# Grouping the scores of the first two quads and the sums of one graph, with six feature blocks moved by ScalarE: a fused graph-attention and relational-attention kernel

## The chip, the core and the metric

The kernel runs on one core of a Trainium2 chip, in one launch. The metric is the device time of that launch in microseconds; less is better. The core has five engines that this document speaks of: TensorE (PE in the profile; PEld is its weight loading), VectorE (DVE), ScalarE (ACT), GpSimd (POOL) and SyncE (SP), which here only issues DMAs. Each works through its own queue in order and waits on semaphores for the others.

## What is computed

Two layers over 64 graphs of 256 nodes with 256 features, all in 32-bit floating point. `adj` holds 0 or 1.

```python
# layer 0: two graph-attention passes, residual, norm, feed-forward, norm
def _gat(h, adj, W, a, n):
    Wh = h @ W
    e = leaky_relu(Wh @ a[:n] + swapaxes(Wh @ a[n:], 1, 2), 0.2)
    return softmax(where(adj > 0, e, -9e15), axis=1) @ Wh
h = _gat(_gat(x, adj, W1, a1, 256), adj, W2, a2, 256)
h = layernorm(x + h) * g_ln1 + b_ln1
x = layernorm(h + relu(h @ w_ff1 + b_ff1) @ w_ff2 + b_ff2) * g_ln2 + b_ln2

# layer 1: eight heads of 32 features; values depend on the relation r = adj
q, k = heads(x @ Wq + bq), heads(x @ Wk + bk)
attn = softmax(q @ k.T / sqrt(32))
out = sum((attn * (adj == r)) @ heads(x @ Wv[r] + bv[r]) for r in range(4))
x1 = layernorm(x + merge(out) @ Wo + bo) * g1 + beta1
x = layernorm(x1 + gelu(x1 @ W1 + b1) @ W2 + b2) * g2 + beta2
```

## The kernel before

The path that runs (`narrow_path`) uses that the adjacency of these inputs holds only 0 and 1, so relational attention needs two value projections. (`general_path` stands in the file for other inputs; it is not run here.) Two graphs make a unit of 512 rows (`G = 2`, `T = 4` tiles of 128 rows), so there are 32 units (`NG`). One call of `turn(y_, x_, z)` works on three units at once: unit `y_` is in relational attention and its feed-forward, unit `x_` in the feed-forward of layer 0, unit `z` in its graph attention. There are 32 turns. In turns 0 to 30 there is a unit `x_` (`X` in the code is true); in turns 1 to 30 the code calls the turn `middle`. In the last turn there is none.

Inside a turn the order of TensorE, SyncE, VectorE and ScalarE is written by hand (`tc.manual_schedule`): each queue holds the instructions in the order of the source. GpSimd's order is left to the scheduler.

Large products use a seven-product scheme in place of eight block products (as Strassen's): a step `2`, `1`, `5`, `3`, `6`, `7` or `4` is one block product, accumulated in PSUM and taken out after each step. What takes it out is ScalarE (a copy) where an output quarter is written first, and VectorE (an add) where the quarter has been begun. This holds for the projections and for the hidden layer:

- `p("q2 v2 q1 ...")` runs steps of the projections of unit `y_`: `q` stands for queries and keys together, `v` for the values. Steps 2, 5 and 3 share one bank, steps 1, 6, 7 and 4 another. The value projections use two banks of their own, with the tags `zo` and `po`. The evictions are on L1040 (VectorE) and L1043 (ScalarE).
- `first("2a 1a ...")` runs steps of the hidden layer of unit `x_`, on halves `a` and `b`. Steps 2, 5 and 3 of a half share the bank `h1b`, steps 1, 6, 7 and 4 the bank `h1a`. The adds are on L909, the copies on L912. `ra`, `rb`, `sa`, `sb` are activations on ScalarE. Steps 5, 6, 7 and 4 need differences of the features, `tt` (L882, four subtractions on VectorE).

PSUM has eight banks of 128 x 512: six of the tag `g`, which `bank()` hands out, and one each of `zo` and `po`.

Attention goes by quads: quad n is four heads of one of the two graphs, so a unit has four quads, 0 and 1 of the first graph, 2 and 3 of the second. For a quad,

- `scores(n)` makes four score tiles on TensorE (L1076, tile `sp`), one bank for each head, with 32 rows of the array for each head, and then calls `powers`;
- `powers(n, heads)` is the exponential on ScalarE (L1085, tile `e`), which frees the bank; `e` and its masked copy `ea` have two buffers each;
- `masks(n)` multiplies by the adjacency on VectorE (L1089, tile `ea`), in two instructions of two heads;
- `totals(n)` adds the two node blocks on VectorE (L1094, tile `es`);
- `sums(n)` makes the weighted values (L1104, tile `po`) and the softmax denominators (L1107, tile `zo`) on TensorE, 32 columns of the array for each head; one bank of each tag serves both quads of a graph;
- `shares(b)` divides, on VectorE (`rz`, `rq`, then L1124), and `out_(b)` is the output projection (`yop`, L812).

In a middle turn TensorE's order around the change is: `q2 v2 q1 v1 q5`, scores 0, `v5 q6 v6 q3 q7 v7 v3 q4 v4`, scores 1, sums 0, `2a 1a 5a`, scores 2, sums 1, scores 3, then `6a 3a` and the other steps of the hidden layer, two products of unit `z` (`xpp`, L741) and step `4b`, sums 2, sums 3, `yop`.

`normed_features` turns a normalized unit into feature-major layout: VectorE transposes blocks of 32 x 32 (`yt`, L694), and 16 blocks of 32 x 256 are then moved between partition groups into `hT`. Four stay in their group (GpSimd). The other twelve are moved by DMAs from SyncE's queue (L714) in the call for layer 0's feed-forward; in the later call for layer 1's feed-forward eight of the twelve are copies by ScalarE (`n % 3 in (1, 2)`).

Other pieces named later: `applied_norm` (L856) is the normalization on ScalarE, four instructions a unit; `offsets` (L846, tile `nm`) prepares its bias; `moments` are the statistics on VectorE (L827, L828); `times` and `plus` (L865, L868) are the scale and shift by the rows `rg` and `rb`; `early(z)` is a transpose for unit `z` (L1135).

Of the kernel before, what the change touches and what calls it, by code (L numbers as in the profile page):

```python
# [9 lines left out]
F32 = mybir.dt.float32  # L10
# [6 lines left out]
P = 128  # L17
# [368 lines left out]
def narrow_path(  # L386
# [13 lines left out]
    nc = tc.nc  # L400
# [8 lines left out]
    T = G * NB  # L409
# [13 lines left out]
    def bank(name):  # L423
        return psum.tile([P, 512], F32, tag="g", name=name, bufs=6)
# [261 lines left out]
        nc.gpsimd.memset(hT[KB - 1][one], 1.0)  # L686
        return hT

    def normed_features(u, l, xn, natural=False, copied=()):


        yt = work.tile([P, Q, KB, T, 32], F32, tag="yt", name=f"yt{u}_{l}", bufs=1)
        for t in range(T):
            mark["transposed"] = nc.vector.transpose(  # L694
                yt[:, :, :, t].rearrange("p q k r -> p k q r"),
                xn[:, t].rearrange("p (k q c) -> p k q c", k=KB, c=32))
        if natural:
            hT = work.tile([P, KB, TN], F32, tag="hT", name=f"hT{u}_{l}")
            to = hT.rearrange("c k (t a r) -> c (k t) a r", a=Q, r=32)
            for q in reversed(range(Q)):  # L700
                for a in range(Q):
                    move = nc.gpsimd.tensor_copy if q == a else nc.sync.dma_start
                    move(to[q * 32:(q + 1) * 32, :, a], yt[a * 32:(a + 1) * 32, q].rearrange("c k t r -> c (k t) r"))
            return with_ones([hT[:, k] for k in range(KB)])
        hT = work.tile([P, Q, KB, T, 32], F32, tag="hT", name=f"hT{u}_{l}")
        n = 0
        for q in range(Q):
            for a in range(Q):
                to, at = hT[q * 32:(q + 1) * 32, a], yt[a * 32:(a + 1) * 32, q]
                if q == a:  # L710
                    nc.gpsimd.tensor_copy(to, at)  # L711
                else:
                    move = nc.scalar.copy if n % 3 in copied else nc.sync.dma_start
                    mark["placed"] = move(to, at)  # L714
                    n += 1
        return [hT[:, :, k].rearrange("p a t r -> p t a r") for k in range(KB)]

    def early_first(z):

# [128 lines left out]
    def applied_norm(y, blocks, mv, rs, nm, part=None, gpsimd=False):  # L848
        if part is None:
            offsets(blocks, mv, rs, nm)  # L850
        for t in part or blocks:
            if gpsimd:
                nc.gpsimd.tensor_scalar(y[:, t, :], y[:, t, :], rs[:, t:t + 1], nm[:, t:t + 1],
                                        op0=ALU.mult, op1=ALU.add)
                continue
            mark["normed"] = nc.scalar.activation(y[:, t, :], y[:, t, :], AF.Identity,  # L856
                                                  bias=nm[:, t:t + 1], scale=rs[:, t:t + 1])
# [6 lines left out]
    def times(y, g_):  # L864
        nc.vector.tensor_mul(y, y, g_[:, None, :].to_broadcast(list(y.shape)))  # L865
# [198 lines left out]

    isd = 1.0 / math.sqrt(DH)

    def weighted(u, b, m, q, k_, aT):


        n = f"{u}_{b}_{m}"  # L1070
        ps = [bank(f"sp{n}_{a}") for a in range(HPB)]
        for j in range(NB):
            j0 = b * N + j * P
            for a in range(HPB):
                hp = slice(a * DH, (a + 1) * DH)
                nc.tensor.matmul(ps[a][:, j * N:(j + 1) * N], k_[hp, m, j0:j0 + P],  # L1076
                                 q[hp, m, b * N:(b + 1) * N], start=True, stop=True)
        e = work.tile([P, HPB, NB * N], F32, tag="e", name=f"e{n}")
        ea = work.tile([P, HPB, NB * N], F32, tag="ea", name=f"ea{n}")
        ab = aT[:, b * NB:(b + 1) * NB, :].rearrange("p t n -> p (t n)")  # L1080
        return ps, (b, m, ab, e, ea)
# [136 lines left out]
    def piece():  # L1218
        if left:
            next(left[0], None)  # L1220

    def turn(y_, x_, z):
# [8 lines left out]
        e, pe = {}, {}  # L1231

        def scores(n, heads=range(HPB)):
            pe[n], e[n] = weighted(y_, *quads[n], q, k_, Y["aT"])
            powers(n, heads)

        def powers(n, heads):
            exps(pe[n], *e[n], heads)

        def masks(n, *pairs):  # L1240
            masked(*e[n], *pairs)

        def totals(n):
            e[n] = node_sums(*e[n])
# [15 lines left out]
            add_blocks(y_, "yop", y, b, lambda t, k: oT[:, k, t * P:(t + 1) * P],  # L1260
                       lambda b, k: wo[:, k, :], KB)

        def first(names, ends=0):

            if X:
                steps(names)
            else:
                for _ in range(ends):
                    piece()


        order = tc.manual_schedule(engines={getattr(mybir.EngineType, n) for n in
                                            ("PE", "SP", "DVE", "Activation")[:4 if X else 2]})
        with order:
# [2 lines left out]
                n = X.pop("n")  # L1277
                offsets(*n)
            middle = X and y_
            p("q2 v2 q1 v1" if middle else "q1 v1 q2")  # L1280
            if middle:
                applied_norm(X["y"], *n, [0, 1, 2, 3])
            elif X:
                applied_norm(X["y"], *n, [0])
            if not middle:
                p("v2")
            if X and not middle:
                applied_norm(X["y"], *n, [1])
            if not middle:
                p("q5")  # L1290
            if X and not middle:
                applied_norm(X["y"], *n, [2, 3])
            if X:
                X["hT"] = normed_features(x_, 0, X["y"])
            if middle:
                p("q5")
                scores(0, (0, 1))
            else:
                scores(0, (0,))
                p("v5")  # L1300
                powers(0, (1,))
            if z + 1 < NG:
                load_x(z + 1)
            if waiting:
                w, wy = waiting[0]
                last = moments(w, 3, wy, range(NB))
            p("v5 q6" if middle else "q3 v3")
            if middle:
                powers(0, (2,))
                p("v6")  # L1310
                powers(0, (3,))
            else:
                powers(0, (2, 3))
            if X:
                masks(0, (0,))
            if middle:
                times(X["y"], rg1)
                p("q3 q7 v7")
                masks(0, (2,))
            else:  # L1320
                p("q6 v6 q7 v7")
                if X:
                    masks(0, (2,))
            if X:
                totals(0)
            else:
                with behind("projected"):
                    masks(0)
                    totals(0)
            while late:  # L1330
                affine(*late.pop(0))
            p("v3 q4 v4" if middle else "q4 v4")
            if waiting:
                last = norm(w, 3, wy, mv=last)
            steps = first_hidden(x_) if X else None
            scores(1)
            masks(1, (0,))
            if waiting:
                offsets(*last)
            masks(1, (2,))  # L1340
            totals(1)
            sums(0)
            if waiting:
                first("2a 1a")
                applied_norm(wy, *last, [0, 1])
                first("5a")
            else:
                first("2a 1a 5a", 1)
            if Z:
                early(z)  # L1350
            scores(2)
            sums(1)
            if waiting:
                applied_norm(wy, *last, [2, 3])
            scores(3, (0, 1, 2))
            first("6a")
            powers(3, (3,))
            if X:
                masks(2)
                totals(2)  # L1360
            first("3a", 1)
            if not X:
                with behind("out"):
                    shares(0)
                masks(2)
                totals(2)
            first("2b ra")
            if X:
                shares(0, [0])
            first("1b 7a")  # L1370
            if X:
                shares(0, [1])
            first("5b sa 6b 4a")
            masks(3, (0,))
            first("3b rb 7b")
            first("sb", 2)
            masks(3, (2,))
            totals(3)
            if X:
                if not middle:  # L1380
                    times(X["y"], rg1)
                plus(X["y"], rb1)
            if Z:
                project(z, range(0, T // 2))
            first("4b")
            sums(2)
            sums(3)
            if not Z:
                shares(1)
            if X:  # L1390
# [51 lines left out]
                Z["m"].scaled(WH)  # L1442
            if Z:
                out.product(6)
                hT = normed_features(y_, 2, y, copied=(1, 2))
                nc.scalar.activation(work.tile([P, 1], F32, tag="ve", name=f"ve{y_}"), mhalf[:, 0:1], AF.Gelu)
                out.add(6)
                out.sums(3)
                out(3)
            elif X:  # L1450
                out.sums(4)
                out(7, 3)
# [191 lines left out]
```

## Time and profile before

| what | value |
|---|---|
| median of 3 runs | 2977.74 us (2977.12 to 2978.61) |
| the profiled execution's own time | 2977.29 us |
| its span | 2975.6 us |
| busy: TensorE | 2936.1 us (99%) |
| busy: VectorE | 2624.7 us (88%) |
| busy: ScalarE | 1822.6 us (61%) |
| busy: GpSimd | 635.6 us (21%) |
| one middle turn | 90.26 us (first projection at 1008.87 us and, a turn later, at 1099.13 us) |
| exponential, 128 x 512, on ScalarE (L1085) | 606 ns, 512 times |
| mask, 128 x 1024, on VectorE (L1089) | 1211 ns, 256 times |
| block move, 32 x 256, on ScalarE (L714) | 402 ns, 240 times |

Times in views are microseconds from the start of the span. A busy time counts an instruction from its start to its end; on VectorE and ScalarE the next instruction may start some 0.1 us before the one ahead is at its end, so the distance from start to start is what a queue advances by. Ends on TensorE are modelled, and its chain lists the distance from one group to the next.

### The profile page before, as it was taken

To read this page: it belongs to the slowest core of one execution; us is meant where nothing else is said; L and a number is where in the kernel's file an instruction comes from. 1 tells how busy PE (TensorE), PEld (TensorE's weight loads), DVE (VectorE), ACT (ScalarE), POOL (GpSimd) and SP (SyncE) were. 2 spreads that over 40 slices of the span, in tenths; PEclk is the share of its full clock that TensorE was granted. 3 is DMA by queue.
4 is the path that set the end of the run, shared out by engine and by line. 5 is a ranking of instruction groups with operands and counts; after the bars stand their busy time and mean duration, and the time that the engine had idled before them with its cause. 6 is when DMAs were issued, how large, how long until landed. Compare 5 with 4: busy or idle time off the path is not lost.

```text
span 2975.6 us, 58457 instructions
## 1 busy us (share of the span) xinstructions
PE 2936.1 (99%) x22192; PEld 2501.2 (84%) x22192; DVE 2624.7 (88%) x5024; ACT 1822.6 (61%) x3803; POOL 635.6 (21%) x930
## 2 busy tenths in 40 slices
PE   7999999999999999999999999999999999999997
PEld 6788888888888888888888888888888888888876
DVE  5788999988999989898989999889999898989886
ACT  4466666656656666666666666666566566666653
POOL 4122121221211221211221212212112212112211
PEclk8999999999999999999999999999999999999999
DMA  5011111111111111111111112111112111111000
GB/s 151 14 32 34 36 33 26 42 35 37 35 34 28 42 35 37 32 26 40 39 35 35 33 26 42 35 36 35 36 26 42 35 37 32 27 38 35 19 10 16
DMA packets 416883, 105.36 MB, mean 35 GB/s; under 512 B 360746, under 2 KB 416084, under 8 KB 416596
## 3 DMA queue, kind: packets, MB, share of 16 engines
q1 hardware_dynamic: 415196, 100.23, 15.5%
q8 instruction: 177, 2.90, 0.4%
q0 software_dynamic: 1056, 1.05, 0.1%
q14 instruction: 110, 0.90, 0.1%
q10 hardware_dynamic: 344, 0.28, 0.0%
HBM read 56.78 MB, written 16.78 MB: 25 GB/s over the span
## 4 chain that ended last, share of the span: by engine, by line
PE 96%; DVE 2%; ACT 1%; DMA 1%; issue 0%; POOL 0%; SPq 0%; POOLq 0%; DVEq 0%; ACTq 0%
PE yf L989 26%; PE h1a L900 15%; PE h1b L900 11%; PE po L1104 8%; PE v L1056 7%; PE qk L1056 6%; PE sp L1076 5%; PE yop L812 4%; PE xpp L741 4%; PE hpp L801 4%; PE ygp L812 3%; PE zo L1107 2%; PE rows L750 1%; DMA wf<-in_L_gnn_w_ff_dram 0%; DVE s L776 0%
## 5 line engine op out<-in xcount | busy, mean ns | idle before, releaser
L1089 DVE TENSOR_TENSOR ea<-e,aT 128x1024 f32<-128x1024 f32 x256 | 307.0, 1211 | 4.2 <-ACT e L1085 4.2
L1085 ACT ACTIVATE e<-sp 128x512 f32<-128x512 f32 x512 | 277.2, 606 | 51.7 <-PE sp L1076 35.8
L856 ACT ACTIVATE y<-y,nm,rs 128x256 f32<-128x256 f32 x450 | 243.1, 596 | 98.9 <-DVE nm L846 94.2
L912 ACT COPY h<-h1b 128x512 f32<-128x512 f32 x262 | 152.7, 583 | 192.7 <-PE h1b L900 191.0
L711 POOL COPY hT<-yt 32x256 f32<-32x256 f32 x244 | 237.4, 973 | 139.0 <-DVE yt L694 131.4
L1043 ACT COPY qk<-qk 128x512 f32<-128x512 f32 x128 | 74.3, 581 | 290.4 <-PE qk L1056 289.0
L918 ACT ACTIVATE h<-h,cols 128x256 f32<-128x256 f32 x512 | 220.8, 498 | 31.4 <-DVE h L909 31.4
L909 DVE TENSOR_TENSOR h<-h1a,h 128x512 f32<-128x512 f32 x262 | 176.2, 682 | 53.1 <-PE h1a L900 43.7
L838 POOL TENSOR_SCALAR rs<-mv 128x4 f32<-128x4 f32 (+1 forms) x134 | 33.9, 253 | 872.4 <-DVE mv L828 296.7
L997 DVE TENSOR_TENSOR y<-yf,y 128x256 f32<-128x256 f32 x448 | 185.5, 414 | 34.0 <-PE yf L989 33.7
L827 DVE BATCH_NORM_STATS2 st<-y 128x6 f32<-128x256 f32 x512 | 208.3, 409 | 5.6
L1117 POOL TENSOR_TENSOR low<-low,rq 128x16 f32<-128x16 f32 x64 | 13.9, 217 | 781.8 <-DVE rq L1116 781.8
L743 ACT COPY xp<-xpp 128x260 f32<-128x260 f32 x128 | 44.2, 368 | 212.0 <-PE xpp L741 211.9
L868 DVE TENSOR_TENSOR y<-y,rb 128x1024 f32<-128x1024 f32 (+1 forms) x130 | 166.0, 1277 | 2.2
L865 DVE TENSOR_TENSOR y<-y,rg 128x1024 f32<-128x1024 f32 (+1 forms) x130 | 162.0, 1246 | 1.2 <-ACT y L856 1.1
L1094 DVE TENSOR_TENSOR es<-e 128x1024 f32<-128x1024 f32 x128 | 155.7, 1217 | 0.0
L1076 PE MATMUL sp<-qk 32*128 32x256 f32 x2048 | 146.6, 400 | 0.0
L1104 PE MATMUL po<-e,v 128*32 128x256 f32 x2048 | 136.3, 384 | 2.1 <-DVE qk L1124 2.1
L839 POOL TENSOR_TENSOR rs<-rs,mhalf 128x4 f32<-128x4 f32 (+1 forms) x134 | 134.6, 1004 | 8.4
L1104 PE MATMUL po<-ea,v 128*32 128x256 f32 x2048 | 134.0, 379 | 0.0
L1076 PEld LDWEIGHTS sp<-qk 32*128 32x128 f32 x2048 | 92.5, 184 | 47.6 <-ACT e L1085 12.8
L900 PE MATMUL h1a<-tt,wf 128*128 128x256 f32 x512 | 131.3, 380 | 0.8 <-DVE h L909 0.8
(284 smaller groups left out, 7783.9 us busy)
## 6 DMA issues: line engine op xcount, KB each, us to landing
hT<-yt SPq DMA_DIRECT2D x852, 32.0 KB, 1.9
y<-in_x_dram SPq DMA_DIRECT2D x32, 512.0 KB, 4.6
xq<-in_x_dram SPq DMA_DIRECT2D x240, 64.0 KB, 2.2
aq<-in_adj_dram SPq DMA_DIRECT2D x240, 64.0 KB, 2.4
out_dram<-y SPq DMA_DIRECT2D x30, 512.0 KB, 2.8
wf<-in_L_gnn_w_ff_dram SPq DMA_DIRECT2D x2, 1024.0 KB, 7.4
w<-in_L_gnn_W_dram SPq DMA_DIRECT2D x2, 1024.0 KB, 7.8
first<-in_adj_dram POOLq DMA_DIRECT2D x2, 512.0 KB, 8.1
```

The costliest lines, as they stand in the source:

```text
L711: nc.gpsimd.tensor_copy(to, at)
L812: nc.tensor.matmul(ps[:, i * F:(i + 1) * F], lhs(t, k), rhs(b, k), start=(k == 0), stop=(k == n - 1))
L827: nc.vector.bn_stats(st[:, t, :], y[:, t, :])
L856: mark["normed"] = nc.scalar.activation(y[:, t, :], y[:, t, :], AF.Identity, bias=nm[:, t:t + 1], scale=rs[:, t:t + 1])
L900: nc.tensor.matmul(ps[:, i * N:(i + 1) * N], w_[:, f * P:(f + 1) * P], m, start=first and i == 0, stop=True, skip_group_check=True)
L918: nc.scalar.activation(y, y if ps is None else ps[:, i * N:(i + 1) * N], func, bias=bi[:, f:f + 1])
L989: nc.tensor.matmul(s.ps[n][:, i * F2:(i + 1) * F2], a[:, k, i * P:(i + 1) * P], w_[:, k, :], start=n in (1, 2, 5) and i == 0 and k == 0, s ...
L1056: nc.tensor.matmul(ps[:, i * N:(i + 1) * N], l, r, start=n in (1, 2, 5) and i == 0, stop=True, skip_group_check=True)
L1076: nc.tensor.matmul(ps[a][:, j * N:(j + 1) * N], k_[hp, m, j0:j0 + P], q[hp, m, b * N:(b + 1) * N], start=True, stop=True)
L1085: nc.scalar.activation(e[:, a, :], ps[a], AF.Exp, scale=isd)
L1089: nc.vector.tensor_tensor(ea[:, a:a + 2, :], e[:, a:a + 2, :], ab[:, None, :].to_broadcast([P, 2, NB * N]), ALU.mult)
L1104: nc.tensor.matmul(po[hp, m * N:(m + 1) * N], vs[:, hp], w[:, a, j * N:(j + 1) * N], start=(n == 0), stop=(n == len(terms) - 1))
```

## The change

1. In turns 0 to 30 the scores of quads 0 and 1 stand together, directly behind all projections. Before, the scores of quad 0 stood between projections. The second quad's third and fourth tile take the banks `zo` and `po`, so both quads together hold all eight.
2. Behind them stand `2a 1a 5a 2b 6a 3a` of the hidden layer, then the scores of quad 2, both sums of the first graph, and the scores of quad 3. Step `4b` stands behind the sums of the second graph.
3. In these turns the exponentials, masks, node sums, norms, `times` and `plus` are placed anew in the queues of ScalarE and VectorE, as the diff shows; `times` and `plus` for unit `x_` stand among the projections.
4. In the call of `normed_features` for layer 0's feed-forward, six of the twelve moves are copies by ScalarE, placed between the evictions of the projections (`moved`), and six stay DMAs. The other call names the same eight copies as before in another form.
5. The last turn is written out on its own; there the third mask and node sum stand ahead of the scores of quad 3, and an output piece with them.

```diff
-    def normed_features(u, l, xn, natural=False, copied=()):
+    def normed_features(u, l, xn, natural=False, copied=(), later=False):
...
-        n = 0
+        n, moves = 0, []
         for q in range(Q):
             for a in range(Q):
                 to, at = hT[q * 32:(q + 1) * 32, a], yt[a * 32:(a + 1) * 32, q]
                 if q == a:
                     nc.gpsimd.tensor_copy(to, at)
                 else:
-                    move = nc.scalar.copy if n % 3 in copied else nc.sync.dma_start
-                    mark["placed"] = move(to, at)
+                    if n not in copied:
+                        nc.sync.dma_start(to, at)
+                    elif later:
+                        moves.append((to, at))
+                    else:
+                        nc.scalar.copy(to, at)
                     n += 1
-        return [hT[:, :, k].rearrange("p a t r -> p t a r") for k in range(KB)]
+        hT = [hT[:, :, k].rearrange("p a t r -> p t a r") for k in range(KB)]
+        return (hT, iter(moves)) if later else hT
...
-    def weighted(u, b, m, q, k_, aT):
+    def weighted(u, b, m, q, k_, aT, last=False):
...
-        ps = [bank(f"sp{n}_{a}") for a in range(HPB)]
+        ps = [psum.tile([P, 512], F32, tag=("zo", "po")[a - 2], name=f"sp{n}_{a}") if last and a > 1
+              else bank(f"sp{n}_{a}") for a in range(HPB)]
...
         def scores(n, heads=range(HPB)):
-            pe[n], e[n] = weighted(y_, *quads[n], q, k_, Y["aT"])
+            pe[n], e[n] = weighted(y_, *quads[n], q, k_, Y["aT"], X and n == 1)
             powers(n, heads)
...
-        def first(names, ends=0):
-
-            if X:
-                steps(names)
-            else:
-                for _ in range(ends):
-                    piece()
-
+        def first(names):
+            steps(names)
+
+        def moved(moves, n):
+            for _ in range(n):
+                nc.scalar.copy(*next(moves))
...
-            p("q2 v2 q1 v1" if middle else "q1 v1 q2")
             if middle:
+                p("q2 v2 q1 v1")
                 applied_norm(X["y"], *n, [0, 1, 2, 3])
-            elif X:
-                applied_norm(X["y"], *n, [0])
-            if not middle:
+                p("q5")
+            else:
+                p("q1 v1 q2")
+                if X:
+                    applied_norm(X["y"], *n, [0])
                 p("v2")
-            if X and not middle:
-                applied_norm(X["y"], *n, [1])
-            if not middle:
+                if X:
+                    applied_norm(X["y"], *n, [1])
                 p("q5")
-            if X and not middle:
-                applied_norm(X["y"], *n, [2, 3])
+                if X:
+                    applied_norm(X["y"], *n, [2, 3])
             if X:
-                X["hT"] = normed_features(x_, 0, X["y"])
-            if middle:
-                p("q5")
-                scores(0, (0, 1))
+                X["hT"], moves = normed_features(x_, 0, X["y"], copied=(1, 3, 5, 7, 9, 11), later=True)
             else:
                 scores(0, (0,))
-                p("v5")
-                powers(0, (1,))
+            p("v5")
             if z + 1 < NG:
                 load_x(z + 1)
             if waiting:
                 w, wy = waiting[0]
                 last = moments(w, 3, wy, range(NB))
-            p("v5 q6" if middle else "q3 v3")
-            if middle:
-                powers(0, (2,))
-                p("v6")
-                powers(0, (3,))
+            if X:
+                moved(moves, 2)
+                p("q6" if middle else "q3")
+                moved(moves, 1)
+                p("v6" if middle else "v3")
+                moved(moves, 3)
+                times(X["y"], rg1)
+                p("q3 q7 v7" if middle else "q6 v6 q7 v7")
+                while late:
+                    affine(*late.pop(0))
+                p("v3 q4 v4" if middle else "q4 v4")
+                plus(X["y"], rb1)
+                if waiting:
+                    last = norm(w, 3, wy, mv=last)
+                steps = first_hidden(x_)
+                scores(0)
+                scores(1, ())
+                first("2a")
+                powers(1, (0, 1, 2))
+                masks(0, (0,))
+                if waiting:
+                    offsets(*last)
+                first("1a")
+                masks(0, (2,))
+                totals(0)
+                first("5a")
+                powers(1, (3,))
+                first("2b")
+                if waiting:
+                    applied_norm(wy, *last, [0, 1])
+                masks(1, (0,))
+                first("6a 3a")
+                masks(1, (2,))
+                totals(1)
+                if waiting:
+                    applied_norm(wy, *last, [2, 3])
+                scores(2, ())
+                sums(0)
+                powers(2, range(HPB))
+                sums(1)
+                first("ra")
+                scores(3)
+                masks(2, (0,))
+                if Z:
+                    early(z)
+                shares(0, [0])
+                first("7a")
+                shares(0, [1])
+                first("sa 1b")
+                masks(2, (2,))
+                totals(2)
+                first("5b 4a 6b 3b")
+                masks(3, (0,))
+                if Z:
+                    project(z, range(0, 1))
+                first("rb 7b")
+                if Z:
+                    project(z, range(1, 2))
+                first("sb")
+                masks(3, (2,))
+                totals(3)
+                sums(2)
+                sums(3)
+                first("4b")
             else:
+                powers(0, (1,))
+                p("q3 v3")
                 powers(0, (2, 3))
-            if X:
-                masks(0, (0,))
-            if middle:
-                times(X["y"], rg1)
-                p("q3 q7 v7")
-                masks(0, (2,))
-            else:
                 p("q6 v6 q7 v7")
-                if X:
-                    masks(0, (2,))
-            if X:
-                totals(0)
-            else:
                 with behind("projected"):
                     masks(0)
                     totals(0)
-            while late:
-                affine(*late.pop(0))
-            p("v3 q4 v4" if middle else "q4 v4")
-            if waiting:
-                last = norm(w, 3, wy, mv=last)
-            steps = first_hidden(x_) if X else None
-            scores(1)
-            masks(1, (0,))
-            if waiting:
-                offsets(*last)
-            masks(1, (2,))
-            totals(1)
-            sums(0)
-            if waiting:
-                first("2a 1a")
-                applied_norm(wy, *last, [0, 1])
-                first("5a")
-            else:
-                first("2a 1a 5a", 1)
-            if Z:
-                early(z)
-            scores(2)
-            sums(1)
-            if waiting:
-                applied_norm(wy, *last, [2, 3])
-            scores(3, (0, 1, 2))
-            first("6a")
-            powers(3, (3,))
-            if X:
-                masks(2)
-                totals(2)
-            first("3a", 1)
-            if not X:
+                while late:
+                    affine(*late.pop(0))
+                p("q4 v4")
+                scores(1)
+                masks(1)
+                totals(1)
+                sums(0)
+                piece()
+                scores(2)
+                sums(1)
+                piece()
                 with behind("out"):
                     shares(0)
                 masks(2)
                 totals(2)
-            first("2b ra")
-            if X:
-                shares(0, [0])
-            first("1b 7a")
-            if X:
-                shares(0, [1])
-            first("5b sa 6b 4a")
-            masks(3, (0,))
-            first("3b rb 7b")
-            first("sb", 2)
-            masks(3, (2,))
-            totals(3)
-            if X:
-                if not middle:
-                    times(X["y"], rg1)
-                plus(X["y"], rb1)
-            if Z:
-                project(z, range(0, T // 2))
-            first("4b")
-            sums(2)
-            sums(3)
+                scores(3)
+                piece()
+                piece()
+                masks(3)
+                totals(3)
+                sums(2)
+                sums(3)
             if not Z:
                 shares(1)
...
-                hT = normed_features(y_, 2, y, copied=(1, 2))
+                hT = normed_features(y_, 2, y, copied=(1, 2, 4, 5, 7, 8, 10, 11))
```

## The prediction

> **What bounds the kernel now.** I read the page first, then the busy time over the steady part, then the chain of one turn, then the queues of the other engines beside it.
>
> From the page, engine totals and the chain that ended last, and below them one row over the steady part (start and end, length, busy of PE, PEld, DVE, ACT, POOL, clock, DMA share, GB/s):
>
> ```profile
> PE 2936.1 (99%) x22192; PEld 2501.2 (84%) x22192; DVE 2624.7 (88%) x5024; ACT 1822.6 (61%) x3803; POOL 635.6 (21%) x930
> ...
> PE 96%; DVE 2%; ACT 1%; DMA 1%; issue 0%; POOL 0%; SPq 0%; POOLq 0%; DVEq 0%; ACTq 0%
> ...
> 300.00:2800.00 2500.00, 2499.95 (x19080) 2137.57 (x19079) 2261.66 (x4314) 1578.92 (x3305) 532.39 (x777) 1.00 0.16 34
> ```
>
> TensorE idles 0.05 us in 2500. So a turn can get shorter only where TensorE itself does its work faster, and any new wait of TensorE is paid in full. The chain of one middle turn, in order of time (start, length, what), shows where TensorE is slower than its own best:
>
> ```profile
> 1464.97 1.08 PE sp L1076 x16
> 1466.05 1.06 PE v L1056 x4
> 1467.11 0.86 PE qk L1056 x4
> ...
> 1474.02 1.08 PE sp L1076 x16
> 1475.09 1.86 PE po L1104 x32
> 1476.96 0.43 PE zo L1107 x8
> 1477.39 1.06 PE h1b L900 x4
> 1478.45 0.86 PE h1a L900 x4
> 1479.31 0.94 PE h1b L900 x4
> 1480.26 1.08 PE sp L1076 x16
> ```
>
> A full-array step (4 records) takes 0.86 us after its like, but 1.06 after scores or after sums. A quad of scores takes 1.08, 0.22 more than such a step; a sum (`po`) takes 1.86 behind scores, and 1.73 behind another sum. Each change of the kind of product costs 0.13 to 0.22 us.
>
> VectorE beside it (busy of PE, PEld, DVE, ACT, POOL), and its queue:
>
> ```profile
> 1474.02:1484.70 10.68, 10.68 (x141) 6.67 (x141) 10.36 (x18) 7.92 (x15) 1.50 (x3) 1.00 0.07 14
> ...
> 1476.39 0.44 DVE L882 TENSOR_TENSOR tt<-hT 128x256 f32<-128x256 f32 x1 [0.22 <-issue]
> ...
> 1477.91 1.21 DVE L1089 TENSOR_TENSOR ea<-e,aT 128x1024 f32<-128x1024 f32 x1
> 1479.04 0.15 DVE L846 SCALAR_TENSOR_TENSOR nm<-mv,rs 128x4 f32<-128x4 f32 x1
> 1479.12 1.21 DVE L1089 TENSOR_TENSOR ea<-e,aT 128x1024 f32<-128x1024 f32 x1
> 1480.25 1.21 DVE L1094 TENSOR_TENSOR es<-e 128x1024 f32<-128x1024 f32 x1
> 1481.39 0.68 DVE L909 TENSOR_TENSOR h<-h1a,h 128x512 f32<-128x512 f32 x1
> ```
>
> VectorE is 97% busy exactly in the stretch that the change rearranges. It stands 1.8 us behind TensorE (the add of 1481.39 belongs to the step of 1478.45, and 1.14 is the least distance), and nobody waits for that today. From start to start a masking or a node sum takes 1.13 us, an add of an eviction 0.60.
>
> **Part 1, regrouping, on TensorE alone.** Call F a full-array step, S a quad of scores, O a quad's sums. From the first score of a turn on, the kinds change as F S F S O F S O S F ... O O F now and as F S S F S O O S F ... O O F after. Extras now, from the chain: S 4 x 0.22, F behind S or O 3 x 0.20, `po` behind another kind 3 x 0.13, `yop` behind O 0.19, and 0.08 in the step of 1479.31: 2.14 us. After: S 3 x 0.22, F 3 x 0.20 (the last is 4b, which now follows the sums), `po` 2 x 0.13: 1.52. That is 0.62 us less a turn. S behind S occurs nowhere in the trace: it costs no less than its weight loads (0.74 in the queue of weight loads) and no more than 1.08; I take 0.86, four products side by side at the pace of F, so +0.22/-0.12 around the 0.62. With 31 turns that have a following group (turns 0 to 30), 31 x 0.62 = 19 us less.
>
> **Part 2, the banks: a new wait.** The two first quads hold all eight banks. Six steps (2a 1a 5a 2b 6a 3a) then take three of them, and the third quad's scores follow. In the built program its four tiles lie in the banks of the first quad's last tile, of the second quad's first two, and of the first half's `h1b`, which 2a, 5a and 3a use. So its fourth matmul waits for the VectorE add of step 3a, the step directly ahead of it. When does that add end? I replay the turn of 1460.65 with the changed orders.
>
> TensorE: 14 projections x 0.864 = 12.10, to 1472.75; S, S and 2a take 0.86 + 1.08 + 1.06 = 3.00, to 1475.75; five more steps 4.32, to 1480.07. The fourth score matmul could start at about 1480.2.
>
> VectorE: v3 is the 11th projection and starts at 1470.16; an add starts 1.14 us after its step (v step at 1470.40, add at 1471.54), so at 1471.30. Behind it, from start to start: the add 0.60; `plus` of rb1 (moved up here) 1.13; two moments and the pause behind them 1.38 (1475.01 to 1476.39); four subtractions for `tt` 1.52; a mask 1.13; `nm` 0.08; the add of 1a 0.60; a mask 1.13; a node sum 1.13; the second quad's first mask 1.13. That is 9.83, and the add of 3a starts at 1481.13. No item of it waits: the first mask needs two exponentials, which are done by 1475.0, and the add of 1a (1477.14) needs a step that TensorE began at 1475.75. ScalarE is nearly as late: exponentials from 1473.91 (start of S plus 1.16), four at 0.49, copy 2a, three exponentials, copy 5a, one exponential, copy 2b at about 0.49 each, two norms 1.06, then copy 6a, done at 1481.0; the add of 3a needs that copy too.
>
> The add ends at 1481.81. The one comparable wait of the trace (TensorE at 2946.86 behind an add of 2946.11) shows a release 0.75 after the add's start, so 1481.88: the fourth score matmul is 1.65 us late. Three matmuls stand ahead of it, but what is left behind it is still a whole group (the fourth head's first, then four more), so I take no credit for them. Queued behind it on TensorE are both sums, the fourth scores and step 7a, all in order. On ScalarE the exponentials of quad 2 now wait for the first sums, since they reuse the buffer that those read (from about 1484.0; behind them stand the two activations of step ra and the exponentials of quad 3), and VectorE's mask of quad 2 waits for these (1485.2). Neither comes back to TensorE: the fourth scores need quad 2's exponentials by 1487.3, and the last is done at 1486.1.
>
> Bounds: nothing, if the add were 1.7 us earlier than replayed (no item of 9.83 can go, but each start may shift); 2.3 if ScalarE's copy of 6a came 0.6 later, the length of one more copy. I take 1.65, the value of the rows.
>
> **Part 3, the rest of the turn.** With TensorE 1.65 later, 7a's add starts at 1489.5, then `rz` 0.73, the division 0.60 and 1b's add, which starts at 1491.4 and releases 6b at 1492.2; TensorE is there at 1491.98. I take 0.25, between 0 and 0.5. The second sums need their node sum at 1494.3 and start later than that; the last node sum ends at 1498.9 and is used at 1500.6. No wait there.
>
> **Part 4, feature blocks.** Six of 12 moves a turn leave SP's queue (12 issues take 7.54 us at 1466.38) for ScalarE: 6 x 0.40 (the row `hT<-yt`, L714) = 2.4 us, while 4 exponentials (2.0) leave that stretch. They stand ahead of copies q6 and v6; q6's copy ends at 1468.0 and q7 needs it at 1468.43, v6's at 1468.9 for 1469.30. So they cost nothing by 0.4 us; without that cover each costs up to 0.4 a turn. The last block lies by 1471.1 at the latest, and `tt` starts at 1474.4. Behind the six DMAs SP holds only `xq` loads, which wait for a later transpose.
>
> **The sum.** Per turn -0.62 + 1.65 + 0.25 = +1.28; x 31 = +39.7 us. On the profiled execution's 2977.29 us (span 2975.6, 1.7 around it; the median of the three runs is 2977.74, 0.45 above) that gives 3017. A measurement here tells about 0.2%, 6 us, from no change.
>
> **Two rules beside this.** "TensorEngine Tiling (Array Packing)" in the Trainium skill, section "Restrictions and Gotchas", warns that row tiling raises the pressure on PSUM, as each row tile needs a bank of its own; it gives no price, and the late bank above is my reading of that price. The gaps of the trace's end leave the clock at 1.00: 16.22 us busy in the 20 us from 2880, PEclk 1.00. "TensorE: Matmul & The Clock Gate", Part 1, says that an idle window of about 3.4 us halves the clock for as long again; by an estimate from that page each stall that tripped it would cost 1.7 us more, 53 us in all, and 3070; a stall of 1.65 stays under it.
>
> **Rivals.** *The bank is free in time*: the regrouping is all that shows, 2977.3 - 19 = 2958. For it: everything on TensorE in part 1 is read off one chain. Against it: the add of 3a would have to start at 1479.4, 1.7 us earlier, in a queue of 9.83 us without a hole. It decides as soon as stall and 6b together are under 0.62 a turn. Chance 0.09. *The stall is about half* (0.5 to 0.8, where starts on VectorE shift): no visible change, 2977. Chance 0.04. *VectorE stays the bound to the end of the turn*: 6b, then the last node sum, which has 1.7 us to spare, come late; at 1 us more a turn, 31 x 2.3 = 71, 3048. For it: VectorE is 88% busy over the span; against it: it has holes behind the stall (1484.0 to 1485.2, 1488.6 to 1489.5). Chance 0.10. The forecast keeps 0.77.
>
> **Range.** Stall 0.9 and no 6b: +0.28, 2986. Stall 2.1 and 6b 0.3: +1.78, 3032. So 2986 to 3033; it leaves out the first rival, the second and most of the third, about 0.2.
>
> **What would show it.** Right: `sp` records twice in a row at 0.86 with no full step between; TensorE idle before L1082 with DVE's add (L914) as releaser, about 50 us over the run; the add of 3a starting about 10 us after that of v3; exponentials of quad 2 waiting for TensorE. Wrong: no idle time before `sp`, or a wait at the projections behind ScalarE's six copies, or at 2a behind feature blocks.

## The result, and the profile after

The changed kernel takes 3020.07 us (median of 4 runs, 3019.72 to 3021.39), the kernel before 2978.18 us on the same chip: ratio 1.0143, 95% interval 1.0130 to 1.0157. The change makes it slower by 42 us; 3017 was predicted, between 2986 and 3033. The profiled execution took 3021.39 us, with a span of 3019.7, 44.1 more than before. One middle turn went from 90.26 us to 91.70 (first projections at 1391.97 and 1483.67). Of the distances from one middle turn to the next, 26 of 29 are within 0.01 us of that; three are longer, by up to 0.24.

First, of the changed kernel, TensorE's share on the page, the steady part (length, busy of PE, PEld, DVE, ACT, POOL, clock, DMA share, GB/s), and the longest entry of TensorE's waits (us in total, times, longest):

```profile
PE 2950.0 (98%) x22192; PEld 2513.9 (83%) x22192; DVE 2619.2 (87%) x5024; ACT 1896.1 (63%) x3989; POOL 627.9 (21%) x930
...
300.00:2800.00 2500.00, 2471.25 (x18780) 2112.88 (x18779) 2219.28 (x4243) 1618.07 (x3411) 513.85 (x761) 1.00 0.15 32
...
PE sp L1082 <- DVE h L914: 28.1, 31, 1.4
```

TensorE, which idled for 0.05 us in the 2500, now idles for 28.75, and 25.0 of that are one wait, in 28 turns (31 over the whole run, once in each turn with a following group): the scores wait for an add of the hidden layer on VectorE. The rest is 0.13 a turn ahead of step 6b, shown below. Then one middle turn on TensorE, its timeline (start, length of the group, idle time ahead in brackets):

```profile
1404.15 2.01 PE L1082 MATMUL sp<-qk 32*128 32x256 f32 x32
...
1410.60 1.03 PE L905 MATMUL h1b<-hT,wf1s 128*128 128x256 f32 x4
1411.56 0.71 PE L1082 MATMUL sp<-qk 32*128 32x256 f32 x6
1413.15 1.13 PE L1082 MATMUL sp<-qk 32*128 32x256 f32 x10 [0.88 <-DVE h L914]
1414.20 1.07 PE L1110 MATMUL po<-e,v 128*32 128x256 f32 x16
...
1422.43 1.03 PE L905 MATMUL h1a<-tt,wf 128*128 128x256 f32 x4
1423.59 1.13 PE L905 MATMUL h1a<-tt,wf1s 128*128 128x256 f32 x4
```

The two first quads stand as 32 records in a row. The third quad breaks off after 6 of its 16 records, three heads of one node block, and goes on 1.59 us later: from its start to the sums it takes 2.64 us, where an unbroken quad takes 1.08. So the sums are 1.56 us late. The idle time in the bracket is only 0.88, since the six records ahead are counted busy; they are no gain, because a whole group's time is still to come. Step 6b starts 1.16 behind 4a in place of 0.86, and the step after it 0.97 later in place of 0.86: 0.40 us.

The releaser, in the same turn: VectorE's timeline, and below it ScalarE's.

```profile
1411.18 1.22 DVE L1095 TENSOR_TENSOR ea<-e,aT 128x1024 f32<-128x1024 f32 x1
1412.41 0.69 DVE L914 TENSOR_TENSOR h<-h1b,h 128x512 f32<-128x512 f32 x1
...
1411.81 0.56 ACT L917 COPY h<-h1a 128x512 f32<-128x512 f32 x1
```

The add of 3a starts 1.23 us behind the mask, where 1.13 is the least distance, and 0.74 us later TensorE goes on. ScalarE's copy of 6a, which the same add needs, ends at 1412.37, 0.04 ahead of it. So both queues are late, and the last is ScalarE, by 0.1 us. This holds in 28 of the 30 middle turns. In two VectorE is the last: in the turn from 1483.67 on, which an expectation below quotes, the copy ended at 1504.07, the add started at 1504.19, directly behind the mask, and the sums were 1.64 late.

### The profile page after: what moved, and what is told of

Its sections match the earlier page's. It is cut to its first block, busy times and chain, and to the rows that moved or that the text cites. A ratio compares the mean times of both kernels' runs of the same rounds, so it can differ in the third digit from the quotient of the medians.

```text
span 3019.7 us, 58640 instructions
## 1 busy us (share of the span) xinstructions
PE 2950.0 (98%) x22192; PEld 2513.9 (83%) x22192; DVE 2619.2 (87%) x5024; ACT 1896.1 (63%) x3989; POOL 627.9 (21%) x930
## 5 line engine op out<-in xcount | busy, mean ns | idle before, releaser
L1091 ACT ACTIVATE e<-sp 128x512 f32<-128x512 f32 x512 | 270.9, 610 | 124.3 <-issue 104.7
L711 POOL COPY hT<-yt 32x256 f32<-32x256 f32 x244 | 211.3, 866 | 138.9 <-DVE yt L694 131.3
L917 ACT COPY h<-h1b 128x512 f32<-128x512 f32 x262 | 157.1, 600 | 120.4 <-PE h1b L905 118.7
L843 POOL TENSOR_SCALAR rs<-mv 128x4 f32<-128x4 f32 (+1 forms) x134 | 42.6, 318 | 857.9 <-DVE mv L833 466.4
L923 ACT ACTIVATE h<-h1a,cols 128x256 f32<-128x256 f32 x256 | 102.7, 465 | 141.8 <-PE h1a L905 141.8
L1082 PE MATMUL sp<-qk 32*128 32x256 f32 x2048 | 159.2, 398 | 28.1 <-DVE h L914 28.1
L1082 PEld LDWEIGHTS sp<-qk 32*128 32x128 f32 x2048 | 103.7, 184 | 78.9 <-DVE h L914 40.6
L905 PE MATMUL h1a<-tt,wf 128*128 128x256 f32 x512 | 137.7, 392 | 0.0
```

What stands on the lines that cost most here:

```text
L917: mark["copied"] = nc.scalar.copy(out(h, o, b), pair(ps))
L923: nc.scalar.activation(y, y if ps is None else ps[:, i * N:(i + 1) * N], func, bias=bi[:, f:f + 1])
L1091: nc.scalar.activation(e[:, a, :], ps[a], AF.Exp, scale=isd)
```

## The experiments

Two theories stood against each other: that TensorE waits for one bank, which is emptied by the eviction of the step directly ahead; and that VectorE as a whole has too much to do there, so that any order of TensorE would wait. A third blames the six moves on ScalarE. Each run is timed beside the kernel before on the same chip (2977.21, 2976.76 and 2976.97 us in the three sets).

**Free the bank by the other engine.** The first of steps 3 and 6 is evicted by ScalarE's copy and the second by VectorE's add, so their order decides who empties `h1b`.

```diff
-                first("6a 3a")
+                first("3a 6a")
```

> The changed kernel with one edit: step 3a of the hidden layer stands ahead of 6a instead of behind it. The bank h1b is then emptied by ScalarE's copy of 3a, and VectorE's add belongs to 6a, whose bank nobody waits for here. Bank theory (TensorE waits for the bank that the add of 3a frees): the copy stands behind the two norms on ScalarE and ends at about 1481.0 in the replay of the prediction, so the wait shrinks from 1.65 to about 0.85 us, and 3a waits some 0.1 for the copy of 5a: 31 x 0.7 = 22 us less than the changed kernel's 3020, about 2998; TensorE's idle time before the scores has ScalarE (L917) as releaser. Rival, VectorE as the bound whatever the bank (it has 9.83 us of work to do before the sums): the wait moves to the sums, the time stays at 3020. Rival, the six moves by ScalarE: 3020 as well.

Measured: 2995.57 us, ratio 1.0059 (1.0042 to 1.0076), 24.5 below the changed kernel. VectorE's work is the same and its add is where it was. That rules out that VectorE's total work sets this wait, and the six moves were not touched. The sign that was expected is not there: TensorE shows no idle time before the scores. But the third quad still takes 1.69 us from its start to the sums (1489.83 to 1491.52), 0.61 more than an unbroken one, and its weight loads wait for ScalarE's copy (L917; 9.1 us in 28 turns).

**And let that copy go ahead of the norms.**

```diff
-                if waiting:
-                    applied_norm(wy, *last, [0, 1])
                 masks(1, (0,))
-                first("6a 3a")
+                first("3a 6a")
+                if waiting:
+                    applied_norm(wy, *last, [0, 1])
```

> The changed kernel with 3a ahead of 6a, and the two norms on ScalarE behind the copy of 3a instead of ahead of it. Bank theory: the copy ends at about 1480.05 in the replay and the fourth score matmul is wanted at 1480.2, so the wait is gone: 31 x (1.65 - 0.1) = 48 us less than 3020, about 2972, below the kernel before. Rival, VectorE as the bound: the sums of quad 1 wait for its second mask and node sum, which do not move; the time stays above 3000. Rival, the six moves: 3020.

Measured: 2980.67 us, ratio 1.0009 (0.9999 to 1.0018): the whole loss is gone, though 9 us more is left than expected. TensorE's timeline of this run:

```profile
1480.84 1.03 PE L905 MATMUL h1b<-hT,wf 128*128 128x256 f32 x4
1481.84 1.13 PE L905 MATMUL h1b<-hT,wf1s 128*128 128x256 f32 x4
1482.80 1.03 PE L905 MATMUL h1a<-tt,wf1s 128*128 128x256 f32 x4
1483.76 1.15 PE L1082 MATMUL sp<-qk 32*128 32x256 f32 x16
1484.84 1.07 PE L1110 MATMUL po<-e,v 128*32 128x256 f32 x16
```

The scores are one group of 16 again, and the sums follow 1.08 behind their start. But 3a starts 1.00 behind 2b and 6a 0.96 behind 3a: 3a now waits for the copy of 5a, and a step that follows a wait costs 0.10 on top. That is 0.23 us a turn where 0.1 had been expected, and the wait that went was 1.56 and not 1.65: 0.22 a turn, some 7 us of the 9.

**And the division behind the add of 1b.**

```diff
-                first("7a")
+                first("7a sa 1b")
                 shares(0, [1])
-                first("sa 1b")
```

> As the run before, and the division of the first graph (two VectorE instructions, 1.3 us) behind the add of step 1b instead of ahead of it. The profile of the changed kernel shows step 6b 0.40 us a turn late behind that add. If that wait is real and nothing else is late next: 31 x 0.40 = 12 us less than the run before, about 2960, and what is left is the regrouping alone, 31 x 0.5 = 16 us below the kernel before (2962). If the division is then late for the second graph's sums, which take over its banks, 2972 or more. VectorE as the bound: no change against the run before.

Measured: 2966.99 us, ratio 0.9964 (0.9950 to 0.9978), 13.7 below the run before: faster than the kernel before. Step 6b starts 0.86 behind 4a, as in this timeline, and nothing else became late (TensorE is busy for all of the 2500 us from 300 to 2800):

```profile
1483.90 1.03 PE L905 MATMUL h1a<-tt,wf 128*128 128x256 f32 x4
1484.76 1.03 PE L905 MATMUL h1a<-tt,wf1s 128*128 128x256 f32 x4
```

**All moves as DMAs.** `copied=()` in place of `copied=(1, 3, 5, 7, 9, 11)` in the changed kernel, and `moved` without anything to move.

> The changed kernel with all twelve moves of feature blocks as DMAs again (no copies by ScalarE among the projections). Bank theory: the moves cost nothing and hide nothing, 3020 within 6. Rival, ScalarE's six copies as a cause of the lateness: 0.61 us of VectorE's idle time before the add of v7 goes, and with it up to 31 x 0.6 = 19 us, 3001. If the twelve DMAs land too late for the steps that now come 2.7 us earlier: above 3030.

Measured: 3079.49 us, ratio 1.0338 (1.0320 to 1.0355). The last of the expected outcomes, and the size was a surprise: the six copies save 59 us in the new order. VectorE's timeline and, below it, TensorE's:

```profile
1529.08 0.43 DVE L887 TENSOR_TENSOR tt<-hT 128x256 f32<-128x256 f32 x1 [2.17 <-DMA hT<-yt]
...
1529.11 1.10 PE L905 MATMUL h1b<-hT,wf 128*128 128x256 f32 x4 [1.48 <-ACT e L1091]
```

VectorE says who is late: the blocks. TensorE's 2a starts at the same moment (ScalarE is named there, but 2a starts 2.33 us behind the start of its exponentials, and in the changed kernel 0.78). So in this order step 2a, which the regrouping brings forward, is not fed in time by twelve DMAs from one queue. Over the steady part its waits make 33.5 us, 38 for 31 turns; the wait of the scores grew from 0.89 to 1.17 us a turn, another 8; and the clock took 17 (see the last section). Together this is about the 63.6 us by which the profiled execution's span, 3083.3 us, exceeds that of the changed kernel.

**The add ahead of the mask, on VectorE alone.**

```diff
-                masks(1, (0,))
                 first("6a 3a")
+                masks(1, (0,))
```

> The changed kernel with one VectorE edit: the add of step 3a stands ahead of the second quad's first mask (1.13 us) instead of behind it. If VectorE alone is the late one, the wait shrinks by up to 0.75 us a turn, 23 us, to 2997. The replay and the profile say that ScalarE's copy of 6a, which the add also needs, ends at 1504.07 in the turn where the add started at 1504.19: then only 0.1 us a turn goes, 3 us, and the time stays at about 3017.

Measured: 3020.24 us, ratio 1.0146 (1.0129 to 1.0163), no change. VectorE's timeline shows why:

```profile
1500.62 0.69 DVE L914 TENSOR_TENSOR h<-h1b,h 128x512 f32<-128x512 f32 x1 [0.98 <-ACT h L917]
```

VectorE now idles for 0.98 us ahead of the add, waiting for ScalarE's copy of 6a. Both queues were late to within 0.1 us of each other, and mending one gives nothing.

**Both queues mended, 3a still behind 6a.** The edit before, and the two norms behind `first("6a 3a")`.

> The changed kernel with both queues mended and 3a behind 6a as it was: the add ahead of the mask on VectorE, and the two norms behind the copy of 6a on ScalarE. Now the add can start when TensorE has made 3a, 1.14 us after that step's start, 0.75 us earlier than before: the wait goes from 1.65 to 0.9 us, 31 x 0.75 = 23 us, 2997. Whatever stays is the length of the eviction behind the step directly ahead. If the wait were of VectorE's total work, moving an instruction within its queue would change nothing: 3020.

Measured: 2999.47 us, ratio 1.0072 (1.0055 to 1.0089), 20.6 below the changed kernel. What stays of the wait is 0.90 us a turn (the third quad takes 1.98 from its start to the sums, 1491.48 to 1493.46): the eviction of the step directly ahead, which no order of the other two queues can shorten, since the add starts at the least distance behind its step, 1.14, in this run. The 23 us against the kernel before are that, 31 x 0.90 = 28, and step 6b, 12, less what the regrouping saves, 16.

**One more mask ahead of the add.** `masks(1, (0,))` twice; the second writes the same values.

> The changed kernel with the second quad's first mask made twice, one more VectorE instruction of 1.13 us a turn ahead of the add of 3a. Bank theory: every microsecond on VectorE there is paid by TensorE, 31 x 1.13 = 35 us, 3055. Rival (the wait has another cause, VectorE has 12% of its span to spare): 3020.

Measured: 3078.14 us, ratio 1.0341 (1.0324 to 1.0359), 58 more instead of 35. The wait itself grew as expected: TensorE idles for 55.5 us in 27 turns of the steady part, 2.06 a turn, where the changed kernel had 25.0 in 28, 0.89; that is 36 us in 31 turns. Of the other 22 us, 20.5 are the clock's, shown in the last section.

**The moves alone, in the kernel before.**

```diff
             p("v5 q6" if middle else "q3 v3")
+            if X:
+                for _ in range(2):
+                    nc.scalar.copy(*next(moves))
...
                 powers(0, (2, 3))
             if X:
+                for _ in range(4):
+                    nc.scalar.copy(*next(moves))
                 masks(0, (0,))
```

> The kernel before with part 4 alone: six of the twelve moves as copies by ScalarE, two behind the eviction of q6 and four behind the exponentials of quad 0 that stand there; scores, sums and steps stay where they were. All theories: 2977 within 6, since the twelve DMAs are hidden in the kernel before and ScalarE has room. If the copies delay the exponentials that the first sums need: above 2985.

Measured: 2987.06 us, ratio 1.0032 (1.0021 to 1.0044), a miss of 10 us. TensorE's timeline:

```profile
1472.78 1.03 PE L1061 MATMUL qk<-tq,wqk 128*128 128x256 f32 x4
1473.82 1.13 PE L1061 MATMUL v<-wv,tq 128*128 128x256 f32 x4
```

Step v7 starts 1.04 behind q7 and the step behind it another 0.97 later: 0.28 us a turn, 31 x 0.28 = 9. The copies stand ahead of the eviction of v6, with the exponentials that are still there in the old order. Room in a queue as a whole does not help the one eviction behind them.

**The price of a change of kind by itself.** In the version of the third run, 4b between the two last sums.

```diff
                 sums(2)
-                sums(3)
                 first("4b")
+                sums(3)
```

> The fastest version so far (3a ahead of 6a, norms and division moved) with step 4b between the second graph's two sums instead of behind them. It measures the price of a change of kind alone: one more entry into sums (0.13) and into a full step (0.20) a turn, no bank and no eviction differs. By the chain of the kernel before: 31 x 0.32 = 10 us above that version's 2967, 2977. If the changes of kind cost nothing in themselves: 2967.

Measured: 2976.03 us, ratio 0.9995 (0.9986 to 1.0004) over 11 runs, 9.0 above that version; one turn takes 90.29 us in place of 89.96. Expected were 10 us and 0.32 a turn: the extras read from the chain are real and add up.

**ScalarE's copy of 5a earlier.** `powers(1, (0, 1))` ahead of it and `powers(1, (2, 3))` behind it, in the version of the third run.

> The fastest version so far, with ScalarE's copy of 5a one exponential earlier (two exponentials of quad 1 ahead of it instead of three). Its profile shows step 3a 0.13 us late a turn behind that copy. If this goes and nothing else comes: 31 x 0.13 = 4 us less than 2967, 2963. If the exponentials are then late for the sums: 2967 or more.

Measured: 2962.16 us, ratio 0.9948 (0.9934 to 0.9962), the fastest version, 15 us below the kernel before. One turn takes 89.83 us. The intervals of this run and of the third overlap, so its 5 us are likely, not shown.

## Why the prediction was right, point by point

**Regrouping, -0.62 a turn: right, a little less.** S behind S cost 0.86 (32 records, and 1.94 us from their start to the next step, as 0.86 + 1.08). The extras of sums and of a full step were confirmed by splitting the sums. But the 0.08 of step 5a did not go: in the changed kernel too the next step starts 0.95 or 0.96 behind it, since 5a waits for the copy of 2a, which moved along. The third version gives the size free of the large wait: 0.30 a turn below the kernel before, with the 0.23 at 3a still in it, so 0.53.

**The bank, +1.65: right, a little less.** 1.56 measured, in 28 of 30 middle turns within 0.01. The add of 3a started 9.88 us behind that of v3 (1402.53 to 1412.41), as in the sum of 9.83. (Step v3 is the 12th projection, not the 11th; the time given for it is right.) ScalarE's copy as the other late one was right too, though it is the last by 0.1 us and not VectorE, as the prediction had it: it took both (20.6 us) where VectorE alone gave nothing. Only the sign to look for was off: 50 us of idle time before `sp` were announced and 28.1 stand there, because of the six records that run ahead.

**Step 6b, +0.25: too small.** It was 0.40. Step 6b itself is 0.30 late, near what was expected; the term left out that the step behind a wait takes 0.97 and not 0.86.

**Feature blocks, 0: right for the changed kernel, and too little said.** No wait of TensorE came from the copies there. The prediction counted the DMAs saved and did not ask whether twelve would still have been in time for a 2a that comes 2.7 us earlier; they would not: with twelve the time is 59 us longer. In the old order the same copies cost 10 us.

**The sum.** -0.52 + 1.56 + 0.40 = 1.44 a turn, where 1.28 was predicted; the profiles show 91.70 - 90.26 = 1.44. Of the difference of 0.16, 6b makes +0.15, 5a +0.10 and the bank -0.09. Times 31 this would be 44.6, and the span grew by 44.1, but not because all 31 turns are alike: the first became 2.7 us longer (92.88 to 95.60, between first projections), and the stretch from the start of the last turn to the end 1.7 shorter (88.67 to 86.95). The prediction worked out neither; that the ends of the run nearly make up for each other is luck.

**The rivals.** A bank free in time gives 2962 to 2967 with two queues reordered; 2958 was worked out for it. A wait of half the size is not seen in any middle turn. VectorE was not the bound to the end of the turn: no wait is seen behind 6b.

**The clock.** In the changed kernel it stays at 1.00, as the prediction had it. Its reason does not hold in general: the last section shows drops behind idle times shorter than the 3.4 us of the page "TensorE: Matmul & The Clock Gate" (Part 1) in the Trainium skill, and the measurement decides.

## What to carry to other kernels

On an engine that is busy all the time, grouping work of one kind saves a little at each border (here 0.13 to 0.22 us), but the buffers that the group holds bind it to the evictions around it: look in the built program which tile reuses which buffer, and replay the queue that empties it up to that instruction, not its busy share. When a buffer is late, see who else would be late at the same place; here VectorE and ScalarE both were, and only moving both (or giving the eviction to the one and clearing its way) paid. A step brought forward must have its inputs brought forward as well.

## What the runs showed of the hardware

The clock of TensorE fell to half behind stalls of about 2 us, in some turns and not in others. The run with the doubled mask, two turns on TensorE's timeline, and below them slices of 3.41 us (length, busy of PE, PEld, DVE, ACT, POOL, clock, DMA share, GB/s), one at the first stall, two at the second:

```profile
1439.73 1.13 PE L1082 MATMUL sp<-qk 32*128 32x256 f32 x10 [2.04 <-DVE h L914]
...
1532.77 1.13 PE L1082 MATMUL sp<-qk 32*128 32x256 f32 x10 [2.21 <-DVE h L914]
...
1438.31:1441.72 3.41, 1.99 (x30) 1.27 (x34) 3.41 (x4) 0.48 (x1) 0.00 (x0) 1.00 0.00 0
...
1530.47:1533.88 3.41, 1.20 (x17) 0.74 (x18) 3.38 (x5) 1.19 (x3) 0.00 (x0) 1.00 0.00 0
1533.88:1537.29 3.41, 3.41 (x37) 1.73 (x40) 1.10 (x1) 1.43 (x3) 0.00 (x0) 0.50 0.00 0
```

Behind the first stall the fourth scores follow 5.51 us later at full clock (1445.24), behind the second 7.20 us later (1539.97). In slices of 2 us from 200 to 2900 us there are 12 such drops, which take 20.5 us, 1.7 each: that is most of what the doubled mask cost beyond its own length. With twelve DMAs there are 10, which take 17.1 us, three of them behind idle times of 0.7 and 1.2 or 1.3 us some 7 us apart. The kernel before and the changed kernel have none in the same stretch.

What decides between a drop and none can be read from the trace of the doubled mask. Each drop lasts 3.41 us, and all start on one raster: from 318.74 to 1533.88, say, is 356 times 3.4133 us. Cut into slices of that raster, TensorE idles 1.59 to 2.21 us in the slice ahead of each of the 12 drops, and at most 1.47 in every other slice from 200 to 2900 us. The stall of 2.04 us lies across a border, with 1.42 us behind 1438.31 and the rest ahead of it; the stall of 2.21 lies within one slice. So in this run it was the place of the stall on the raster, and not its length alone. With twelve DMAs the drops lie on such a raster too, but the idle time of the slice does not tell them apart: 1.15 to 2.17 us ahead of a drop, and up to 1.68 without one. That stays open.
